# The last batch element: output projection by token halves, its first half two value groups sooner, x in halves, and the last output block in two pieces

## The chip, the cores and the metric

The kernel runs on one core of a Trainium2 chip. The core has a matrix engine (TensorE, "PE" in the profile, with its weight loads as "PEld"), a vector engine (VectorE, "DVE"), a scalar engine (ScalarE, "ACT"), GpSimd ("POOL") and a queue engine (SyncE, "SP") that issues nearly all DMAs here. The engines run side by side, each in its own program order, and wait for each other through semaphores. The metric is the device time of one execution in microseconds (us), as the median over runs.

## What is computed

The input x has 8 batch elements of 512 channels and 32 x 32 = 1024 tokens, in float32. Each element goes through two layers.

```python
# layer 0: group norm, 8-head attention, output projection, group norm, residual
hn  = group_norm(x, gn1_scale, gn1_bias)                       # 32 groups
qkv = einsum('bchw,oc->bohw', hn, w_qkv) + b_qkv
q, k, v = split(qkv.reshape(b * 8, 3 * 64, n))
wgt = softmax(einsum('bct,bcs->bts', q * s, k * s))            # s = 64 ** -0.25
a   = einsum('bts,bcs->bct', wgt, v)
out = einsum('bchw,oc->bohw', a, w_proj) + b_proj
x   = x + group_norm(out, gn2_scale, gn2_bias)
# layer 1: weight-normed attention over tokens, one head of 512 channels
qkv = einsum('oc,bcn->bon', w_qkv, x);  qkv = qkv / (rms(qkv) + 1e-4)
attn = softmax(einsum('bci,bcj->bij', q, k) * 512 ** -0.5)
x   = (x + w_out @ (attn @ v)) * 2 ** -0.5
```

## The kernel before

Channels lie on the 128 partitions in `CI = 4` blocks of 128, tokens in the free dimension; `HN = 512` is half of the tokens. The elements are worked through one after another, and most of what would leave PE idle in one element is filled with work of the next. The last element, b = 7, has no next one, so it has code of its own (the `else` branches of `if more`).

*The attention of layer 0* (`Heads`). The 8 heads are taken in pairs, a pair for each channel block j, and each pair in 8 steps of 128 query tokens, 32 steps in all (`STEPS`). In a step PE makes scores (`s`), DVE takes their maximum, ACT the exponential, POOL scales the rows. One step later `turn` transposes the probabilities on DVE (`pb`, 2.3 us) and issues four DMAs on SP, 256 KB each, that put them in a tile `pT` of the group. Two steps make a group; `values(g)` is the product of the group's `pT` with v (`po`, 32 matmul records of 64 x 256), and ACT copies its result into 256 columns of `a`. A pair has four groups, so groups 12 and 13 are the first half of the tokens of the last pair, and 14 and 15 the second half. Group 13 is taken in the last step, 14 and 15 after it.

*The output projection of the last element.* Output block j is the sum over the four input blocks ci of `proj[ci, j]` times `a[ci]`. `project_out_half` makes the part of ci = 0 and 1 during the last pair's steps, and leaves it in `o`. After `values(14)` and the last `turn`, `OutBegun` makes the part of ci = 2 for j = 0 to 2 in three double-bank PSUM tiles `pp` (tag "sc", three buffers, shared with the scores). `finish_last` adds the part of ci = 3 behind `values(15)`, makes j = 3, and per j DVE adds the tile to `o` over 1024 columns, takes two statistics of 512 columns each (`bn_stats`) and aggregates them. `GroupNorm` turns them into a scale and a shift per channel: two tiny matmuls (`pm`, `pv`) that average over a group, and some twenty small DVE operations. Then for each j ACT scales `o[:, j, :]` and DVE adds it into x, each over 1024 columns. Every matmul of the projection appears as two records in the profile.

*DMAs around it.* SP holds, in this order: the last `turn`'s four DMAs, `score` (weights of layer 1), blocks 2 and 3 of x, then `gram` and `value`. `gram` goes into the buffer in which `proj` lies, so its DMA waits for the last `pp`.

*Layer 1* (`Layer1`). `py` multiplies `gram` with x, block by block, for the norm of q, k and v; `p_u`, `p_v` and `p_e` follow, then `po` (here 128 x 512) with `esum` as the denominators. `products(th, c)` makes output block c of token half th, and `keep` multiplies it by the denominators' reciprocals on DVE, adds x, and for th = 1 issues the whole block's DMA to the output (128 x 1024, 512 KB).

*Buffers.* `Slots` hands out seven large SBUF slots in the order in which they were given back. `wide` takes a double-bank PSUM tile, `bank` a single-bank one (tag "mm", two buffers).

Of the kernel before, what the change touches and what calls it, by code (L numbers as in the profile page):

```python
# [8 lines left out]
F32 = mybir.dt.float32  # L9
I32 = mybir.dt.int32  # L10
AF = mybir.ActivationFunctionType
ALU = mybir.AluOpType
AX = mybir.AxisListType
P = 128
# [4 lines left out]
G1S, G1B, BQ, BK, BV, BP, G2S, G2B, GQKV, GOUT, NCOLS = 0, 4, 8, 12, 16, 20, 24, 28, 32, 44, 48  # L19
# [6 lines left out]
class InOrder:  # L26


    def __init__(self, tc, engine):
        self._pin, self._engine = tc.keep_in_program_order, engine  # L30
# [22 lines left out]
def attention_blocks_kernel(  # L53
# [26 lines left out]
    B, C, H, W = x.shape  # L80
    N = H * W
    NH, D, GROUPS = 8, C // 8, 32
    CI, NT, HN = C // P, N // P, N // 2
# [6 lines left out]
    ov = out.rearrange("b (ci p) h w -> b p ci (h w)", p=P)  # L90

    const = ctx.enter_context(tc.tile_pool(name="const", bufs=1))
    slots = Slots(ctx.enter_context(tc.tile_pool(name="slots", bufs=1)), "s", 7)
# [5 lines left out]
    small = ctx.enter_context(tc.tile_pool(name="small", bufs=3))  # L99
# [4 lines left out]
    PE, VE, AC, PO, SY = (InOrder(tc, e) for e in (nc.tensor, nc.vector, nc.scalar, nc.gpsimd, nc.sync))  # L104

    def big(name, lead=CI):

        return slots.take([P, lead, CI * N // lead], name)

    def wide(name):  # L110
        return ps_s.tile([P, 2, HN], F32, tag="sc", name=name)
# [4 lines left out]
    def matmuls(pm, terms):  # L116

        for k, (lhsT, rhs) in enumerate(terms):
            PE.matmul(pm, lhsT, rhs, start=(k == 0), stop=(k == len(terms) - 1))
            if k % 2:  # L120
                yield

    def run(pieces):
        for _ in pieces:
            pass
# [24 lines left out]
    def load_x(b, xt, ci):  # L150
        SY.dma_start(out=xt[:, ci, :], in_=xv[b, :, ci, :])
# [35 lines left out]
    cols = const.tile([P, NCOLS], F32, name="cols")  # L187
# [18 lines left out]
    def rsqrt(r, v, n, name):  # L206
# [11 lines left out]
    far = {  # L218
        name: dram.tile(shape, F32, tag=f"far_{name}", name=f"far_{name}")
        for name, (_, shape) in places.items()  # L220
        if name not in ("qk", "t24", "qk7", "v", "spare")
    }
# [3 lines left out]
    near = {}  # L226
    far_rinv = dram.tile([NT, P], F32, tag="far_rinv", name="far_rinv")

    def place(name, b):
        tag, shape = places[name]  # L230
        near[name] = weights.tile(shape, F32, tag=f"w_{tag}", name=f"{name}_{b}")
        if name == "v":

            near["v7"] = near[name]
            flat = near[name].rearrange("p k h c -> p (k h c)")
            near["v#"], near["v_"] = flat[:, CI * C :], flat[:, : CI * C]
            near[name] = flat[:, : CI * C].rearrange("p (ci c) -> p ci c", ci=CI)
        return near[name]
# [13 lines left out]
    def fetch(name, b):  # L252
        SY.dma_start(out=place(name, b), in_=far[name])
# [16 lines left out]
    def gn_stats(st, src, k):  # L270
        VE.bn_stats(st[:, k, :], src[:, k * HN : (k + 1) * HN])

    class GroupNorm:


        def __init__(self, mv, n, g0, b0, name, bank=bank):
            self.mv, self.n, self.g0, self.b0, self.name, self.bank = mv, n, g0, b0, name, bank
# [238 lines left out]
    def project_v7(b, right, v):  # L516

        w = near["v7"]

        def unit(m):  # L520
            c = {f"{i + 1}{th + 1}": v[:, m + 4 * th, i * CH : (i + 1) * CH] for i in range(2) for th in range(2)}
            return Seven(
                f"v0_{b}_{m}", CH,
                lambda k, h: w[:, k, h, :], right(slice(m * P, (m + 1) * P)), c, lambda which: None, swap=True,
            ).steps()

        for m in (0, 2):
            units = [unit(m), unit(m + 1)]
            for _ in range(7):
                for u in units:  # L530
                    next(u)
                    yield
# [97 lines left out]
    def out_terms(a, j, th, cis):  # L630
        hs = slice(th * HN, (th + 1) * HN)
        return [(near["proj"][:, ci, j * P : (j + 1) * P], a[:, ci, hs]) for ci in cis]
# [7 lines left out]
                AC.activation(o[:, j, th * HN : (th + 1) * HN], pm, AF.Identity, bias=col(BP, j))  # L640
            yield

    class OutBegun:


        def __init__(self, b, h):
            self.pm = {}
            for j in range(CI - 1):
                self.pm[j] = wide(f"pp_{b}_{j}")
                for th in range(2):  # L650
                    for lhsT, rhs in out_terms(h.a, j, th, [CI // 2]):
                        PE.matmul(self.pm[j][:, th, :], lhsT, rhs, start=True, stop=False)

    def finish_last(b, h, xt, o, begun):

        def project_out(j, th, pm):
            terms = out_terms(h.a, j, th, range(CI // 2, CI))
            if j in begun.pm:  # L660
                PE.matmul(pm[:, th, :], *terms[1], start=False, stop=True)
            else:
                run(matmuls(pm[:, th, :], terms))

        st = small.tile([P, CI, 2, 6], F32, tag="gn_st2", name=f"st2_{b}")
        mv = small.tile([P, CI, 2], F32, tag="gn_mv2", name=f"mv2_{b}")
        for j in range(CI):
            pm = begun.pm[j] if j in begun.pm else wide(f"pp_{b}_{j}")
            for th in range(2):
                project_out(j, th, pm)  # L670
            VE.tensor_add(o[:, j, :], o[:, j, :], pm.rearrange("p a f -> p (a f)"))
            for k in range(2):
                gn_stats(st[:, j], o[:, j, :], k)
            VE.bn_aggr(mv[:, j, :], st[:, j])
        fetch("gram", b)
        norm = GroupNorm(mv, CI, G2S, G2B, f"2_{b}")
        norm.means()
        a, c = norm.coeffs()
        for j in range(CI):
            AC.activation(o[:, j, :], o[:, j, :], AF.Identity, bias=c[:, j : j + 1], scale=a[:, j : j + 1])  # L680
            VE.tensor_add(xt[:, j, :], xt[:, j, :], o[:, j, :])
        slots.give(f"a_{b}")
        slots.give(f"o_{b}")

    class RightSide:

# [197 lines left out]
    class Layer1:  # L884
# [172 lines left out]
        def keep(self, th, c):  # L1057
# [6 lines left out]
            if th == 1:  # L1064
                SY.dma_start(out=ov[self.b, :, c, :], in_=self.xt[:, c, :])

# [2 lines left out]
    gram = place("gram", 0)  # L1072
# [79 lines left out]
    score, value = done1[:, :CI, :], done1[:, CI:, :]  # L1152
# [45 lines left out]
    heads, norm1, hn_next = Heads(0, x0, v0_0, qk0), None, None  # L1198
# [3 lines left out]
    for b in range(B):  # L1202
        hn, more = heads.hn, b + 1 < B
        todo, due, rest = iter(()), [], []
        for i in range(STEPS):
            j, r = divmod(i, NB)
# [13 lines left out]
            if r == 0:  # L1220
# [6 lines left out]
                if j + 1 == CI:  # L1227
                    slots.give(f"hn_{b}")
                    if not more:
                        o_last = big(f"o_{b}")  # L1230
# [5 lines left out]
            if not b:  # L1236
# [9 lines left out]
                k = i - 3 * CI - 2  # L1246
# [16 lines left out]
            if more and m >= 0:  # L1263

                if m < 2:
                    k = slice(2 * (i - STEPS + NB), min(2 * (i - STEPS + NB) + 2, 7))
# [7 lines left out]
            if not more and i == STEPS - 4:  # L1274
                xt = big(f"x_{b}")
# [4 lines left out]
        if more:  # L1280
            v0_next = big(f"v0_{b + 1}", NT)
            v0 = project_v7(b + 1, right_v.columns, v0_next)
            Seven.hold()
            for _ in range(4):
                next(v0)
        heads.values(STEPS // RG - 2)
        heads.turn()
        if more:
            Seven.drain()
            fetch("proj7", b)  # L1290
            ta = big(f"ta_{b}").rearrange("p (k i) (h n) -> p k i h n", k=2, h=2)
            rhs = RightSide(heads.a, ta[:, 0], ta[:, 1])
            for j in range(CI // 2 + 1):
                rhs.sums(j)
            for _ in range(10):
                next(v0)
        else:
            fetch("score", b)
            begun = OutBegun(b, heads)
            for ci in (2, 3):  # L1300
                load_x(b, xt, ci)
        heads.values(STEPS // RG - 1)
        slots.give(f"v0_{b}")
        if more:
            xt = big(f"x_{b}")
            for ci in range(CI):
                load_x(b, xt, ci)
            fetch("gram", b)
            finish_layer0(b, heads, rhs, xt, v0)
        else:  # L1310
            finish_last(b, heads, xt, o_last, begun)
        fetch("value", b)
        one = Layer1(b, xt)
        one.project(hn_next)
# [27 lines left out]
        if more:  # L1342
            one.products(1, 0, norm_step)
            run(steps)
            one.keep(1, 0)
            heads = Heads(b + 1, hn_now, v0_next, qk_next)
            heads.scores(0)
            fills = [[lambda c=c: one.products(1, c)] for c in range(1, CI)] + [[]]
            laters = [[lambda c=c: one.keep(1, c)] for c in range(1, CI)] + [[]]

            def done(b=b):
                for name in (f"v1_{b}", f"e_{b}_1", f"x_{b}"):
                    slots.give(name)

            laters[CI - 2].append(done)
        else:
            for c in range(CI):
                one.products(1, c)
                one.keep(1, c)


# [31 lines left out]
```

## Time and profile before

| what | value |
| --- | --- |
| time, median of 3 runs | 3246.95 us (3246.25 to 3247.75) |
| the profiled execution: time / span of its core | 3249.17 / 3246.7 us |
| granted TensorE clock, mean | 0.998 |
| PE busy | 3217.5 us (99%), 13346 matmul records |
| DVE busy | 2274.4 us (70%) |
| ACT busy | 1045.7 us (32%) |
| POOL busy | 1253.0 us (39%) |
| PE, DVE, ACT busy in 3056 to 3068 us | 2.01, 8.75, 2.69 of 12 us |

How to read it: the span is the time from the first to the last instruction of the core; the execution's own time is 2.47 us longer. The profile's pages give groups by engine and operation as "out<-in", with the mean duration of one in ns. The chain of waits follows the work that ended last back from the last instruction, at each step to what released it. A timeline row has its start and duration in us, the engine, the operation, its tiles and shapes, a count where equal instructions were merged, and in brackets the idle time before it with what ended it. Nearly all operations are recorded on line 34 (a helper), so tiles tell them apart. Matmul ends are modelled.

### The profile page before, as it was taken

What the parts mean: (1) busy time and instruction counts of PE and PEld (TensorE: products, weight loads), DVE (VectorE), ACT (ScalarE), POOL (GpSimd) and SP (SyncE); (2) the same over time, 40 slices, a digit from 0 to 9 for tenths busy, and PEclk for the clock granted to TensorE, in tenths of its full rate; (3) what the DMA queues carried; (4) which work ended last, traced back from release to release, by engine and by line L of the source; (5) the groups of instructions that cost most, each with busy time, mean ns of one, the idle gap of its engine ahead of it and who ended that gap; (6) DMA issues with size and microseconds to landing.
All of it is one profiled execution on the core that took longest, in us unless ns stands there. A gap on an engine that the chain in (4) does not pass through costs nothing.

```text
span 3246.7 us, 36723 instructions
## 1 busy us (share of the span) xinstructions
PE 3217.5 (99%) x13346; PEld 1657.8 (51%) x13346; DVE 2274.4 (70%) x3074; ACT 1045.7 (32%) x1813; POOL 1253.0 (39%) x1025
## 2 busy tenths in 40 slices
PE   8999999999999999999999999999999999999899
PEld 5445644455444554445544555445554456444454
DVE  5697667876678756886668866687667876578643
ACT  2453114521145211551215412254123531145210
POOL 1554224732257212671227603265223642246121
PEclk9999999999999999999999999999999999999999
DMA  6776215862168511784228822388214872158500
GB/s 201 213 203 209 75 49 155 219 193 59 49 183 229 171 43 56 202 229 138 52 77 214 229 96 63 95 219 242 78 49 115 216 214 75 23 157 210 183 7 26
DMA packets 231579, 447.34 MB, mean 138 GB/s; under 512 B 28996, under 2 KB 69480, under 8 KB 225512
## 3 DMA queue, kind: packets, MB, share of 16 engines
q1 hardware_dynamic: 231280, 444.97, 49.0%
q8 instruction: 107, 1.75, 0.2%
q14 instruction: 72, 0.59, 0.1%
q10 hardware_dynamic: 120, 0.02, 0.0%
HBM read 133.06 MB, written 29.52 MB: 50 GB/s over the span
## 4 chain that ended last, share of the span: by engine, by line
PE 93%; DMA 3%; DVE 2%; SPq 1%; issue 1%; POOL 0%; DVEq 0%
PE po L34 26%; PE s L34 13%; PE pq L34 7%; PE p_e_T L34 7%; PE p_v_T L34 6%; PE p_e_B L34 5%; PE p_v_B L34 5%; PE py L34 4%; PE pqk L34 4%; PE p_u_T L34 3%; PE p_o_T L34 3%; DMA pT<-pb 3%; PE p_u_B L34 3%; PE p_o_B L34 2%; SPq L34 1%; DVE pb L34 1%
## 5 line engine op out<-in xcount | busy, mean ns | idle before, releaser
L34 POOL TENSOR_SCALAR p<-p,tt 128x1024 f32<-128x1024 f32 x512 | 565.9, 1118 | 753.7 <-DVE tt L34 734.9
L34 ACT ACTIVATE p<-s,nm 128x1024 f32<-128x1024 f32 x512 | 565.7, 1109 | 887.7 <-DVE nm L34 794.1
L34 DVE TENSOR_REDUCE nm<-s 128x1 f32<-128x1024 f32 x512 | 602.0, 1217 | 158.9 <-PE s L34 158.6
L34 DVE STREAM_TRANSPOSE pb<-p 128x2048 f32<-128x2048 f32 x256 | 589.6, 2303 | 45.6 <-DMA pT<-pb 20.8
L34 PE MATMUL s<-qk 64*128 64x512 f32 x2048 | 526.5, 604 | 0.6
L34 PE MATMUL po<-pT,v 128*64 128x256 f32 x4096 | 471.7, 383 | 3.5 <-DMA pT<-pb 3.4
L34 PE MATMUL po<-e,v 128*128 128x512 f32 x1024 | 451.7, 595 | 0.0
L34 PEld LDWEIGHTS po<-pT,v 128*64 128x64 f32 x4096 | 285.9, 137 | 220.8 <-ACT v L34 32.6
L34 PEld LDWEIGHTS s<-qk 64*128 64x128 f32 x2048 | 199.5, 186 | 253.3 <-issue 227.9
L34 PEld LDWEIGHTS po<-e,v 128*128 128x128 f32 x1024 | 191.9, 190 | 245.0 <-issue 236.4
L34 POOL TENSOR_TENSOR u<-u,xy 128x512 f32<-128x512 f32 x64 | 78.9, 1270 | 335.4 <-DMA xy<-far_rinv 261.4
L34 PE MATMUL pq<-hn,qk 64*128 64x512 f32 x504 | 197.1, 592 | 0.0
L34 POOL TENSOR_TENSOR esum<-esum,e 128x512 f32<-128x512 f32 x96 | 130.5, 1360 | 154.2 <-ACT e L34 151.7
L34 POOL TENSOR_TENSOR x<-x,o 128x1024 f32<-128x1024 f32 x21 | 52.1, 2512 | 348.3 <-ACT o L34 348.3
L34 ACT ACTIVATE e<-e,shift,rinv 128x512 f32<-128x512 f32 x128 | 100.9, 812 | 256.6 <-DVE e L34 256.6
L34 DVE TENSOR_TENSOR e<-e,p_e_T 128x512 f32<-128x512 f32 x160 | 106.9, 684 | 86.5 <-PE p_e_T L34 84.3
L34 DVE TENSOR_TENSOR v<-v,p_v_T 128x256 f32<-128x256 f32 x300 | 114.2, 415 | 68.7 <-PE p_v_T L34 50.0
L34 PE MATMUL pqk<-hn,qk 64*128 64x512 f32 (+1 forms) x672 | 158.2, 590 | 0.0
L34 PE MATMUL pq<-t,qk 64*128 64x512 f32 x336 | 150.9, 589 | 0.0
L34 PE MATMUL pq<-v,qk 64*128 64x512 f32 x336 | 150.9, 589 | 0.0
L34 PE MATMUL p_e_T<-s,t 128*128 128x512 f32 x320 | 147.8, 592 | 0.0
L34 PE MATMUL py<-x,gram 128*128 128x512 f32 x320 | 140.2, 597 | 5.4 <-issue 5.4
(215 smaller groups left out, 4130.9 us busy)
## 6 DMA issues: line engine op xcount, KB each, us to landing
pT<-pb SPq DMA_DIRECT2D x1024, 256.0 KB, 4.4
qk<-far_qk SPq DMA_DIRECT2D x21, 896.0 KB, 8.6
hn<-in_x_dram SPq DMA_DIRECT2D x32, 512.0 KB, 5.8
x<-in_x_dram SPq DMA_DIRECT2D x32, 512.0 KB, 4.5
out_dram<-x SPq DMA_DIRECT2D x32, 512.0 KB, 3.8
score<-far_score SPq DMA_DIRECT2D x8, 1792.0 KB
value<-far_value SPq DMA_DIRECT2D x8, 1792.0 KB, 7.2
proj<-far_proj SPq DMA_DIRECT2D x7, 1792.0 KB
```

The lines of the kernel that those rows point to most:

```text
L34: return lambda *args, **kw: self._pin(call(*args, **kw))
```

## The change

All of it concerns the last element.

1. `LastOut` takes the place of `OutBegun` and `finish_last`. Its PSUM tiles hold two output blocks of one token half instead of two halves of one block. `first_half` makes the parts of ci = 2 and 3 for tokens 0 to 511, right after `values(13)` and ahead of `values(14)`. `sums` adds one block's half to `o` and takes its statistic: for block 0 it stands ahead of the last `turn` on DVE, for blocks 1 to 3 behind it. `begin_second` makes the part of ci = 2 of the second half ahead of `values(15)`, and `finish` the part of ci = 3 behind it, then the four remaining sums, the aggregates and the norm.
2. ACT's scaling and DVE's addition into x go by halves of 512 columns.
3. `gram` goes into one of the seven slots, and its DMA is issued ahead of x's blocks 2 and 3 and `score`.
4. The last output block's first half is sent on its own; its second half is made, scaled and sent in two pieces of 256 columns.

```diff
-    class OutBegun:
...
-    def finish_last(b, h, xt, o, begun):
...
+    class LastOut:
+        def __init__(self, b, h, o):
...
+        def two(self, th, js):
+            t = wide(f"pp_{self.b}_{th}_{js[0]}")
+            for k, j in enumerate(js):
+                self.pm[th, j] = t[:, k]
+        def share(self, th, j, ci, first):
+            for lhsT, rhs in out_terms(self.h.a, j, th, [ci]):
+                PE.matmul(self.pm[th, j], lhsT, rhs, start=first, stop=not first)
+        def first_half(self):
+            for js in ((0, 1), (2, 3)):
+                self.two(0, js)
+                for j in js:
+                    self.share(0, j, CI - 2, True)
+                    self.share(0, j, CI - 1, False)
+        def sums(self, th, j):
+            oh = self.o[:, j, th * HN : (th + 1) * HN]
+            VE.tensor_add(oh, oh, self.pm[th, j])
+            VE.bn_stats(self.st[:, j, th, :], oh)
+        def begin_second(self):
+            for js in ((0, 1), (2, 3)):
+                self.two(1, js)
+                for j in js:
+                    self.share(1, j, CI - 2, True)
+        def finish(self, xt):
+            for j in range(CI):
+                self.share(1, j, CI - 1, False)
+            for j in range(CI):
+                self.sums(1, j)
+                VE.bn_aggr(self.mv[:, j, :], self.st[:, j])
+            norm = GroupNorm(self.mv, CI, G2S, G2B, f"2_{b}")
+            norm.means()
+            a, c = norm.coeffs()
+            for j in range(CI):
+                for th in range(2):
+                    hs = slice(th * HN, (th + 1) * HN)
+                    AC.activation(
+                        o[:, j, hs], o[:, j, hs], AF.Identity, bias=c[:, j : j + 1], scale=a[:, j : j + 1]
+                    )
+                    VE.tensor_add(xt[:, j, hs], xt[:, j, hs], o[:, j, hs])
...
+        def last_piece(self, c, cols):
+            hs, po = slice(HN + cols.start, HN + cols.stop), bank(f"po1_{self.b}_1_{c}_{cols.start}", HN // 2)
+            run(matmuls(po, [(self.v[:, t, c * P : (c + 1) * P], self.e[1][:, t, cols]) for t in range(NT)]))
+            VE.tensor_mul(po, po, self.sums[1][:, cols])
+            VE.scalar_tensor_tensor(self.xt[:, c, hs], self.xt[:, c, hs], 2.0 ** -0.5, po, ALU.mult, ALU.add)
+            SY.dma_start(out=ov[self.b, :, c, hs], in_=self.xt[:, c, hs])
...
+        else:
+            last = LastOut(b, heads, o_last)
+            last.first_half()
+            last.sums(0, 0)
         heads.values(STEPS // RG - 2)
         heads.turn()
...
         else:
-            fetch("score", b)
-            begun = OutBegun(b, heads)
+            for j in range(1, CI):
+                last.sums(0, j)
+            last.begin_second()
+            near["gram"] = big(f"gram_{b}")[:, :, :C]
+            SY.dma_start(out=near["gram"], in_=far["gram"])
             for ci in (2, 3):
                 load_x(b, xt, ci)
+            fetch("score", b)
         heads.values(STEPS // RG - 1)
...
-            finish_last(b, heads, xt, o_last, begun)
+            last.finish(xt)
...
-            for c in range(CI):
+            for c in range(CI - 1):
                 one.products(1, c)
                 one.keep(1, c)
+            SY.dma_start(out=ov[b, :, c + 1, :HN], in_=xt[:, c + 1, :HN])
+            for n in (0, HN // 2):
+                one.last_piece(c + 1, slice(n, n + HN // 2))
```

More of the change, by code (lines that the diff above doesn't have):

```diff
@@ L641, in project_out_half @@
             yield
-    class OutBegun:
-        def __init__(self, b, h):
-            self.pm = {}
-            for j in range(CI - 1):
-                self.pm[j] = wide(f"pp_{b}_{j}")
-                for th in range(2):
-                    for lhsT, rhs in out_terms(h.a, j, th, [CI // 2]):
-                        PE.matmul(self.pm[j][:, th, :], lhsT, rhs, start=True, stop=False)
-    def finish_last(b, h, xt, o, begun):
[L658 to L683, printed above, removed]
@@ new lines, in attention_blocks_kernel @@
+    class LastOut:
+        def __init__(self, b, h, o):
+            self.b, self.h, self.o = b, h, o
+            self.st = small.tile([P, CI, 2, 6], F32, tag="gn_st2", name=f"st2_{b}")
+            self.mv = small.tile([P, CI, 2], F32, tag="gn_mv2", name=f"mv2_{b}")
+            self.pm = {}
+        def two(self, th, js):
[21 more added lines that the diff above has]
+        def finish(self, xt):
+            b, o = self.b, self.o
+            for j in range(CI):
[7 more added lines that the diff above has]
+            for j in range(CI):
+                for th in range(2):
+                    hs = slice(th * HN, (th + 1) * HN)
[3 more added lines that the diff above has]
+                    VE.tensor_add(xt[:, j, hs], xt[:, j, hs], o[:, j, hs])
+            slots.give(f"a_{b}")
+            slots.give(f"o_{b}")
```

## The prediction

> **What bounds the kernel now.** I read the page first, then the chain of waits over the last 250 us, then the timeline of single engines where that chain leaves PE. By the page, the chain that ended last is
>
> ```profile
> PE 93%; DMA 3%; DVE 2%; SPq 1%; issue 1%; POOL 0%; DVEq 0%
> ```
>
> So TensorE sets the time, and a change that takes no matmul away can gain only where the chain is not on PE. The chain over the last batch element shows one such place that is long (columns: start us, duration us, what):
>
> ```profile
> 3044.29 3.67 PE po L34 x32
> 3047.97 1.93 PE pp L34 x4
> 3049.89 0.02 issue
> 3049.92 1.23 DVE o L34
> ...
> 3060.44 0.22 DVE mv L34
> ...
> 3062.53 5.38 issue
> 3067.91 18.88 PE py L34 x40
> ```
>
> From 3049.92 to 3067.91 us the chain is DVE and ACT: no later element is left whose work could fill PE. Of these 18.0 us, 10.7 are the sums of the output projection and their statistics (3049.92 to 3060.66), 4.65 the group norm's small operations, and 2.60 the scaling and the first addition into x. The DVE timeline shows what one of four channel blocks costs, and how long DVE stood idle just before:
>
> ```profile
> 3034.35 2.31 DVE L34 STREAM_TRANSPOSE pb<-p 128x2048 f32<-128x2048 f32 x1 [2.34 <-POOL p L34]
> 3049.92 1.22 DVE L34 TENSOR_TENSOR o<-o,pp 128x1024 f32<-128x1024 f32 x1 [13.25 <-PE pp L34]
> ...
> 3057.91 1.17 DVE L34 TENSOR_TENSOR o<-o,pp 128x1024 f32<-128x1024 f32 x1
> 3059.11 1.29 DVE L34 BATCH_NORM_STATS2 st<-o 128x6 f32<-128x512 f32 x2
> 3060.44 0.21 DVE L34 BATCH_NORM_AGGREGATE mv<-st 128x2 f32<-128x12 f32 x1
> ```
>
> From py on, PE is busy without a break to the last matmul (chain, 3067.91 to 3241.52). Behind it only this tail counts:
>
> ```profile
> 3241.54 0.70 DVE L34 TENSOR_TENSOR po<-po,esum 128x512 f32<-128x512 f32 x1 [5.45 <-PE po L34]
> 3242.27 0.69 DVE L34 SCALAR_TENSOR_TENSOR x<-x,po 128x512 f32<-128x512 f32 x1
> 3242.99 0.33 SPq L34 DMA_DIRECT2D out_dram<-x  x1
> ```
>
> The span ends at 3246.70, 3.71 us after that DMA's issue.
>
> **Part 1: half of the sums leave the chain (−4.4 us).** DVE now does, per block, an addition over 1024 columns (1.20 us to the next start), two statistics (1.32) and an aggregate (0.13), 2.65 us, four times. After the change, first-half additions and statistics stand before the last values group, in the idle 13.25 us above: four additions of 128x512 (0.69, the x<-x,po row) and four statistics (0.68, the row's mean), 5.6 us with their gaps. What is left is, per block, 0.72 + 0.71 + 0.13 = 1.56 us, with the last aggregate 6.32 us. 10.74 − 6.32 = 4.42 us.
>
> **Part 2: what the move costs in front (+1.9 us).** The 32 pp matmul records after group 13 stay 32; 16 of them now stand before group 14, 8 before group 15, 8 at the end. Group 13 starts at 3027.29 and holds PE 3.61 us (the step from one group to the next matmul elsewhere), so the first pp starts at 3030.90 in a gap that PE now spends waiting for group 14's transposed tile ([2.83 <-DMA pT<-pb] at 3033.80). At 0.43 us a record, with 0.11 for ACT's copy of group 13 (ready 3031.48), 16 records end at 3037.9; with 0.19 at each change of operand group 14 starts at 3038.1, long after its tile, and the 8 further records at 3041.7. PE can start group 15 at 3045.3, against 3044.29: **+1.0**.
>
> The catch is DVE's order. The addition for block 0 stands before the last transpose on DVE, and in the instruction order of the changed kernel it waits for the last of the four products of its PSUM tile, blocks 0 and 1 both. These 8 records end at 3034.6; the addition and its statistic hold DVE until 3036.0, so the transpose starts at 3036.0 instead of 3034.35. Queued behind it are its four SP DMAs, and group 15 waits for those. Before, the last of them landed 7.5 us after the transpose ended (3044.20, just ahead of the 3044.29 start); for the transpose before that it took 6.4. So the tile lands between 44.8 and 45.9. I take PE's 3045.3, because the earlier transpose's DMAs, which shared the engines with these, will by then be done; the upper end adds 0.6.
>
> At the end the same pairing counts: block 0's addition must wait for four records behind ACT's copy of group 15, not two: 2 × 0.43 = **+0.86**. DVE's sums then start at 3045.3 + 5.63 + 0.86 = 3051.8 and end at 3058.1, 2.5 us earlier than now.
>
> **Part 3: x in halves (−1.1 us).** ACT's first scaling takes 1.23 us and DVE follows 0.05 later; a 128x512 ACT operation takes 0.63 to 0.81 in this trace (squares, exponentials), so I take 0.70. DVE's addition goes from 1.22 to 0.68, and py starts 0.10 after it: 0.75 + 0.68 + 0.10 = 1.53 instead of 2.60. The other seven pieces come every 0.7 us while py's first matmuls are slow (below), so PE does not wait for them. py starts at 3064.4, 3.5 us earlier.
>
> **Part 4: the last block in two pieces (−1.4 us).** PE's share is unchanged: 128x256 matmuls step by 0.215 us (p_v: 16 in 3.45), 512-wide ones by 0.43. The last two DVE operations become 256 wide (0.42, the p_v additions): 1.42 to 0.87 us. The last DMA carries 128 KB instead of 512. Its 128 packets, eight on each engine, shrink from 4 KB (0.159 us in the packet records) to 1 KB (between 0.027 for 512 B and 0.084 for 2 KB, so 0.045): about 0.9 of 3.71 us. Bounds: 0 (all of it fixed) and 1.3. The two earlier pieces and block 2 leave SP 3 us or more ahead.
>
> **Free edits.** gram goes to a slot that group 13 frees, and is issued first, then x's blocks 2 and 3, score and value: 5.8 MB. At 292 GB/s (what 3036 to 3048 moved) gram and x are in by 3051, score by 3058, value by 3064; first uses are near 3064, 3083 and 3109. Landing at 3068 instead would cost 3.6 us.
>
> **The sum.** +1.02 + 0.86 − 4.42 − 1.07 − 1.42 = −5.0 us. The profiled execution has a span of 3246.70 and a time of 3249.17, which becomes 3244.2; the median of the runs, 2.2 us below it, goes from 3246.95 to 3242.0 (−0.15%).
>
> **The clock.** After PE's idle stretch, weights for py's first records come every 0.86 us, then every 0.43:
>
> ```profile
> 3067.88 0.50 PEld L34 LDWEIGHTS py<-x,gram 128*128 128x128 f32 x2 [5.45 <-issue]
> 3068.90 0.34 PEld L34 LDWEIGHTS py<-x,gram 128*128 128x128 f32 x1 [0.52 <-issue]
> ...
> 3071.18 0.19 PEld L34 LDWEIGHTS py<-x,gram 128*128 128x128 f32 x1 [0.24 <-issue]
> ```
>
> These 3.0 slow us cost 1.5 (18.72 us from py to p_u_B, against 40 × 0.43 = 17.2). The sum leaves them as they are. [...]
>
> **Rivals.**
> A, the slow stretch of py shrinks: at most 1.5 us more, together with an early landing in the tail (0.4 more) 6.9 saved, 3240.0. [...] Against: PE is idle about as long before py as now.
> B, it grows by as much: 3.5 saved, 3243.5. [...]
> C, the change does not do what it says: the first-half sums slip behind group 15 because DVE or PSUM is late, and nothing is gained but the tail and x halves: 2.5 − 1.9 saved, 3246.3. Against: 13.25 idle us of DVE, and PSUM tiles whose readers end 1 us before they are wanted.
> D, slower: group 15's tile. The transpose is 1.7 us late and gram and x now follow its DMAs directly. If their 2.1 MB (7.2 us at 292 GB/s) shared the engines with it instead of following, the tile would land at 3044.8 + 7.2 = 3052.0, 6.7 after PE is ready, and a PE idle that long would run group 15 slow as it ran group 14 (5.11 us in the chain against 3.67): −5.0 + 6.7 + 1.4 = 3.1 slower, 3250.1. It decides from a landing at 3049 on. For it: the 2.83 us wait for group 14 shows such tiles can be late. Against: score's 1.8 MB followed the same DMAs before, and group 15 did not wait.
>
> **Numbers.** Forecast 0.68 (3240.6 to 3243.0), A 0.14, B 0.11, C 0.04, D 0.03. The range 3240.0 to 3244.2 takes in the bounds of parts 2 and 4 and both clock cases, and leaves out C, D and the far ends. A change of 0.2%, about what a measurement of this kernel can tell from none, is 6.5 us: faster by more than that is A and the best edge of the forecast, 0.17; slower is D where it is worse than worked out, 0.02; within it the rest, 0.81.
>
> **What would show it.** Right: pp x16 directly behind group 13 with no wait for pT before group 14; the last transpose near 3036.0; DVE's last sums 6.3 us long, starting near 3051.8; py near 3064.4; last DVE operations of 0.42 and less than 3 us behind the last issue. Wrong: a transpose at 3034.4 (the pairing is not real), a wait for pT before group 15 over 0.6 us, first-half sums after group 15, py waiting for gram, or a py stretch other than 18.7 us.

## The result and the profile after

Over 20 runs of each kernel the median went from 3249.26 us (3245.87 to 3253.99) to 3244.38 us (3241.66 to 3249.58). The ratio is 0.9986, with a 95% interval of 0.9979 to 0.9992: 4.5 us faster, 2.6 to 6.8. The forecast was −5.0 us, −0.15%, so the difference lies where it was put. The time itself does not: 3244.38 is 0.2 us above the range given, because the kernel before is not at 3246.95, the median of the three runs shown, but 2.3 us higher.

The profiled execution of the changed kernel has a span of 3243.2 us and a time of 3245.3. Its chain over the last element (start us, duration us, what):

```profile
3030.69 7.06 PE pp L34 x16
3037.75 3.60 PE po L34 x32
3041.36 3.63 PE pp L34 x8
3044.99 0.76 issue
3045.74 3.69 PE po L34 x32
...
3049.98 2.00 PE pp L34 x4
...
3052.01 0.70 DVE o L34
...
3058.02 0.22 DVE mv L34
...
3063.02 0.82 ACT o L34
...
3063.87 0.70 DVE x L34
...
3064.61 19.91 PE py L34 x40
```

PE goes straight from group 13 into pp and has no gap ahead of group 14. There is a new one, 0.76 us, ahead of group 15; the last transposed piece of its tile lands at 3045.65 by the trace's DMA records, so the nameless wait is a DMA's. DVE's last sums run from 3052.01 to 3058.24, 6.2 us instead of 10.7. py comes 3.3 us sooner, but takes longer: 19.75 us to p_u_B instead of 18.72.

The DVE timeline shows why group 15's tile is late:

```profile
3034.36 0.69 DVE L34 TENSOR_TENSOR o<-o,pp 128x512 f32<-128x512 f32 x1 [2.62 <-PE pp L34]
3035.08 0.69 DVE L34 BATCH_NORM_STATS2 st<-o 128x6 f32<-128x512 f32 x1
3035.69 2.29 DVE L34 STREAM_TRANSPOSE pb<-p 128x2048 f32<-128x2048 f32 x1
```

DVE waits 2.62 us for pp, and the transpose stands behind that: it starts 8.7 us after group 13 instead of 7.1. In the tail, the last two DVE operations and the last issue are

```profile
3239.31 0.43 DVE L34 TENSOR_TENSOR po<-po,esum 128x256 f32<-128x256 f32 x1 [2.56 <-PE po L34]
3239.78 0.42 DVE L34 SCALAR_TENSOR_TENSOR x<-x,po 128x256 f32<-128x256 f32 x1
3240.23 0.33 SPq L34 DMA_DIRECT2D out_dram<-x  x1
```

and the span ends at 3243.22, 2.99 us behind that issue (3.71 before).

### The profile page after: what moved, and what is told of

It reads as the page before. It is cut to its first block, busy times and chain, and to the rows that moved or that the text cites. A ratio compares the mean times of both kernels' runs of the same rounds, so it can differ in the third digit from the quotient of the medians.

```text
span 3243.2 us, 36769 instructions
## 1 busy us (share of the span) xinstructions
PE 3216.9 (99%) x13362; PEld 1662.9 (51%) x13362; DVE 2277.4 (70%) x3084; ACT 1047.8 (32%) x1817; POOL 1254.4 (39%) x1025
## 4 chain that ended last, share of the span: by engine, by line
PE 93%; DMA 3%; DVE 2%; SPq 1%; issue 0%; POOL 0%; ACT 0%; DVEq 0%; ACTq 0%
PE po L34 26%; PE s L34 13%; PE p_e_T L34 7%; PE pq L34 7%; PE p_v_T L34 6%; PE p_e_B L34 5%; PE p_v_B L34 5%; PE py L34 4%; PE pqk L34 4%; PE p_u_T L34 3%; PE p_o_T L34 3%; PE p_u_B L34 3%; DMA pT<-pb 2%; PE p_o_B L34 2%; DVE pb L34 1%; SPq L34 1%
## 5 line engine op out<-in xcount | busy, mean ns | idle before, releaser
L34 PE MATMUL po<-e,v 128*128 128x512 f32 (+1 forms) x1040 | 451.7, 589 | 0.0
```

The costliest lines, as they stand in the source:

```text
L34: return lambda *args, **kw: self._pin(call(*args, **kw))
```

## The experiments

All of them leave the part ahead of group 13 of the last element as it was. So each profile gives two numbers: when group 13 starts, and the *stretch*, from there to the end of the span. The stretch is 219.4 us in the profile of before, and 216.2 in that of the change.

**The kernel before, again.** No edit.

> The kernel before, unchanged. Theory 1 (the forecast's steps were right and its starting level was low: executions of this kernel differ by several us, and three of them gave a median on the low side): a ratio of 1.000 within 0.001, single times spread over 3246 to 3254 us, and a profile in which the stretch from the start of values group 13 of the last element to the last DVE operation is the 215.7 us of the earlier profile within 1.5 us, while the start of group 13 may lie anywhere from 3025 to 3034 us. Rival (the level is steady and the loss was in the changed stretch): single times within 1.5 us of 3247, group 13 starts within 0.5 us of 3027.3.

Measured: ratio 1.0002 (0.9993 to 1.0011), single times 3246.7 to 3252.8; the kernel before had a median of 3249.0 over 33 runs beside it. In the profile group 13 starts at 3024.09, 3.2 us sooner than in the first, and the stretch is 220.2. The rows of PE at the place of the change:

```profile
3030.39 3.67 PE L34 MATMUL po<-pT,v 128*64 128x256 f32 x32 [2.63 <-DMA pT<-pb]
...
3040.65 3.67 PE L34 MATMUL po<-pT,v 128*64 128x256 f32 x32 [1.24 <-DMA pT<-pb]
```

Theory 1 holds: the level moves, and it moves ahead of the changed code (group 13 is even 0.9 us outside the band that was named for it). In the twelve profiles of this study group 13 starts between 3024.09 and 3031.60 us, 7.5 us apart, with the same instructions in front of it. Note the second row: in the kernel before, too, group 15 can wait for its tile.

**The tail alone.** The kernel before with `last_piece` as in the change, and its calls:

```diff
...
-            for c in range(CI):
+            for c in range(CI - 1):
                 one.products(1, c)
                 one.keep(1, c)
+            SY.dma_start(out=ov[b, :, c + 1, :HN], in_=xt[:, c + 1, :HN])
+            for n in (0, HN // 2):
+                one.last_piece(c + 1, slice(n, n + HN // 2))
```

> The kernel before with the last output block in two pieces and nothing else of the change. By the forecast: last DVE operations 0.87 us instead of 1.42, from the last DMA's issue to the end of the span 2.8 instead of 3.7, together 1.4 us sooner, ratio 0.9996. Rival (the DMA's time is fixed whatever its size): 0.55 us sooner, the span ending 3.7 us behind the issue.

Measured: ratio 0.9996 (0.9988 to 1.0005), which alone cannot be told from no change. The profile can: last DVE operations 0.89 us instead of 1.42, and from the last issue at 3243.42 to the end of the span 2.70 us instead of 3.71. Together that is 1.5 us, and the fixed-time rival is out. The stretch is 218.2.

**x in halves alone.**

```diff
-            AC.activation(o[:, j, :], o[:, j, :], AF.Identity, bias=c[:, j : j + 1], scale=a[:, j : j + 1])
-            VE.tensor_add(xt[:, j, :], xt[:, j, :], o[:, j, :])
+            for th in range(2):
+                hs = slice(th * HN, (th + 1) * HN)
+                AC.activation(o[:, j, hs], o[:, j, hs], AF.Identity, bias=c[:, j : j + 1], scale=a[:, j : j + 1])
+                VE.tensor_add(xt[:, j, hs], xt[:, j, hs], o[:, j, hs])
```

> The kernel before with ACT's scaling and DVE's addition into x by halves and nothing else. By the forecast: from ACT's first scaling to py's first matmul 1.5 to 1.6 us instead of 2.60, py itself 18.7 us if its slow stretch keeps its length; 1.0 us sooner, ratio 0.9997. Rival (the eight pieces hold up py): py's stretch to p_u_B grows by 1 us or more because PE waits for later pieces of x, and nothing is gained. Rival (the granted clock decides): py's stretch takes any length from 17.2 to 20 us, according to where the half-clock stretch ends, with no wait for DVE behind its fourth matmul.

Measured: ratio 0.9995 (0.9987 to 1.0004); from ACT's first scaling to py 1.64 us instead of 2.60, and py to p_u_B 19.04. Weight loads come every 0.86 us until 3068.84 and every 0.43 from 3069.31 on, so the later pieces of x hold nothing up; the end of the slow stretch does not follow them. The third theory fits. The stretch is 217.9, 1.5 to 2.2 less than before, but 0.4 to 0.9 of that is group 15, which starts 16.14 us behind group 13 here (17.0 and 16.56 in the two profiles of before). The edit does not touch that part: here group 15 waits 0.67 us for its tile, in the second profile of before 1.24, and in the first it does not wait, but group 14 takes 5.11 us instead of 3.67, 3.0 of them at half clock (3033.34 to 3036.75 by the clock records).

**The projection alone.** The changed kernel with the loops of the kernel before for x and the tail.

> The changed kernel without x in halves and without the two-piece tail: the projection by token halves and gram's own slot alone. By the forecast's steps with what the changed kernel's profile showed: group 15 starts 18.5 to 18.8 us behind group 13 instead of 17.0, DVE's last sums take 6.2 us instead of 10.7 and start 6.3 us behind group 15 instead of 5.6; py starts 2.3 to 2.6 us sooner relative to group 13, ratio 0.9992. Rival (the late transpose eats the gain): py starts less than 1 us sooner relative to group 13, ratio 1.000.

Measured: ratio 0.9993 (0.9984 to 1.0002). Group 15 starts 18.58 us behind group 13 and now waits for a DMA by name:

```profile
3050.18 3.67 PE L34 MATMUL po<-pT,v 128*64 128x256 f32 x32 [0.60 <-DMA pT<-pb]
```

The sums start 6.26 us behind it and take 6.2; py starts 38.29 us behind group 13, against 40.62 and 40.20: 1.9 to 2.3 us, at or a little under the lower end of what was expected. The stretch is 217.2. The three ratios of the parts, 0.9996, 0.9995 and 0.9993, add up to 0.9984, the whole measured 0.9986; each of the three is uncertain by 0.0009, so what each part is worth is read from its profile.

**The transpose first.**

```diff
             last.first_half()
-            last.sums(0, 0)
...
-            for j in range(1, CI):
+            for j in range(CI):
                 last.sums(0, j)
```

> The changed kernel with the sums of block 0's first half behind the last transpose on DVE instead of ahead of it. Theory (the late transpose makes group 15's tile late): the transpose starts 7.0 to 7.2 us behind group 13's start as in the kernel before (8.7 in the changed kernel), group 15 starts when PE is free, 18.0 to 18.1 us behind group 13 instead of 18.7, and the stretch from group 13's start to the end of the span falls from 216.2 to about 215.5 us. Rival (the DMAs behind the tile, gram and x, hold it up): group 15 still waits and starts 18.5 us or more behind group 13 with the transpose at 7.1.

Measured: ratio 0.9983 (0.9974 to 0.9991). DVE's and PE's rows:

```profile
3032.18 2.31 DVE L34 STREAM_TRANSPOSE pb<-p 128x2048 f32<-128x2048 f32 x1 [2.35 <-POOL p L34]
...
3043.02 3.67 PE L34 MATMUL po<-pT,v 128*64 128x256 f32 x32
```

The transpose is back at 7.1 us behind group 13 (3025.11), where POOL ends its wait as before, and group 15 starts at 17.9 with no wait, though only just: the last piece of its tile lands at 3042.92 by the DMA records. So the 0.6 to 0.8 us there came from the order on DVE, not from gram or x. The stretch is 214.7, 0.8 below the expectation, of which py's length explains 0.7 (19.04 instead of the 19.75 that was counted on).

**Own PSUM tiles for blocks 0 and 1.**

```diff
-            for js in ((0, 1), (2, 3)):
+            for js in ((0,), (1,), (2, 3)):
                 self.two(0, js)
...
-            for js in ((0, 1), (2, 3)):
+            for js in ((0,), (1,), (2, 3)):
                 self.two(1, js)
```

> The changed kernel with blocks 0 and 1 of each half in PSUM tiles of their own, so that an addition waits for its own block's products alone. Theory (both costs in front come from the shared tile): the transpose starts 7.0 to 7.2 us behind group 13, group 15 18.0 to 18.1 us, DVE's last sums start 5.6 us behind group 15 instead of 6.26; group 13 to the end of the span about 214.9 us instead of 216.2. Rival (group 15 waits for the DMAs anyway, or PSUM is short with six tiles in three buffers): only the 0.6 us at the sums, or PE waits for DVE ahead of group 15.

Measured: ratio 0.9974 (0.9964 to 0.9985). DVE's and PE's rows (group 13 starts at 3026.92):

```profile
3032.54 0.69 DVE L34 TENSOR_TENSOR o<-o,pp 128x512 f32<-128x512 f32 x1 [0.91 <-PE pp L34]
...
3033.98 2.31 DVE L34 STREAM_TRANSPOSE pb<-p 128x2048 f32<-128x2048 f32 x1
...
3044.82 3.67 PE L34 MATMUL po<-pT,v 128*64 128x256 f32 x32
```

The first addition starts 5.6 us behind group 13 instead of 7.4 and the transpose 7.06; group 15 starts at 17.9 without a wait; the last sums start 5.41 us behind it (0.2 sooner than expected). The stretch is 214.8 as expected, although py met its longest slow time, 20.03. Against the change: group 15 0.8 sooner, the sums 0.85, py 0.3 longer.

**PE kept busy.** Nine products that nobody reads:

```diff
+            idle = wide(f"idle_{b}")
+
+            def keep_busy(n):
+                for _ in range(n):
+                    PE.matmul(idle[:, 0], near["proj"][:, 0, :P], self.h.a[:, 0, :HN], start=True, stop=True)
+
+            keep_busy(5)
             norm = GroupNorm(self.mv, CI, G2S, G2B, f"2_{b}")
             norm.means()
             a, c = norm.coeffs()
+            keep_busy(4)
```

> The changed kernel with nine more products of 128x512 into a spare PSUM tile that nobody reads, five behind the last pp and four behind pv: work that stands in PE's idle time and changes no output. Theory (the granted clock falls to half in that idle time, and py starts in it): no half-clock stretch there, py to p_u_B 17.2 to 17.6 us instead of 19.75 in the changed kernel's profile (18.7 to 19.9 in the others), py no later than now; group 13 to the end of the span 213.7 to 215.0 us instead of 216.2. Rival (the slow first py matmuls wait for x in pieces, not for the clock): py to p_u_B stays over 18.7 us. Rival (the added products are in the way): pm, pv or py start later by 0.5 us or more.

Measured: ratio 0.9980 (0.9971 to 0.9989). PE's rows:

```profile
3053.82 4.46 PE L34 MATMUL idle<-a,proj 128*128 128x512 f32 x10
3058.68 0.36 PE L34 MATMUL pm<-mv,gavg 128*128 128x4 f32 x2 [0.40 <-DVE mv L34]
3059.77 0.36 PE L34 MATMUL pv<-d,gavg 128*128 128x4 f32 x2 [0.73 <-DVE mean L34]
3059.98 3.68 PE L34 MATMUL idle<-a,proj 128*128 128x512 f32 x8
3064.51 17.43 PE L34 MATMUL py<-x,gram 128*128 128x512 f32 x40 [0.85 <-DVE x L34]
3081.78 1.88 PE L34 MATMUL p_u_B<-x,score 128*128 128x512 f32 x4
```

py to p_u_B is 17.27 us, the 40 × 0.43 of full speed, and the mean granted clock of the run is 1.0 instead of 0.998. The records of pm and pv shrink too, 0.36 us instead of 0.56, and from pm's second record to ACT's scaling it takes 4.14 instead of 4.45. The stretch is 213.1, 0.6 below the expectation's lower end, which had left pm and pv out. x in pieces is not what slows py's start: with the granted clock at 1.0, py's weight loads come every 0.43 us from 3065.91 on.

**Both together.**

> Both of the last two: own PSUM tiles for blocks 0 and 1, and PE kept busy behind the last pp and behind pv. If the two costs are independent, group 13 to the end of the span is 212.5 to 213.5 us (216.2 less 1.3 and less 1.5 to 2.4), ratio to the kernel before 0.9979 with the spread of the part ahead of group 13 on top, so 0.997 to 0.999. Rival (they overlap, since an earlier py meets another clock state): no better than the better one alone.

Measured: ratio 0.9970 (0.9959 to 0.9982), median 3240.17 us of 6 runs beside 3248.62. Stretch 211.9, 7.5 to 8.3 below the kernel before and 3.4 to 4.3 below the change. That is 0.6 under the expected range, again by pm and pv. Against the first profile of the change 4.3 us are saved. The two edits alone save 1.7 (own tiles, with py's length left out) and 3.1 (PE kept busy), so the two costs are nearly independent. Some 0.3 us are lost again: pm starts 0.45 us behind the last aggregate instead of 0.14, directly behind the idle products, of which five are too many once the sums end sooner. This version is the fastest of the study by ratio and by stretch; against the change as it stands the two intervals overlap, and the claim rests on the stretch.

**gram in its old place.** The changed kernel with `fetch("gram", b)` behind the sums, `score` and x ahead of it, as before the change.

> The changed kernel with gram back in proj's buffer, so that its DMA waits for the last pp and stands behind score and x. Theory (the forecast: gram's move costs and brings nothing, its cover is wide): gram is issued near 27 us behind group 13's start and lands 5 us later, py still waits for DVE's x alone; group 13 to the end of the span as in the changed kernel, 215.2 to 217 us. Rival (py waits for gram): py's idle time ends with a DMA, 1 us or more later. Rival (gram's packets held up group 15's tile): group 15 starts 18.0 us behind group 13 instead of 18.5 to 18.7.

Measured: ratio 0.9982 (0.9973 to 0.9991), gram issued at 3052.31, 26.5 us behind group 13. py's wait still ends with DVE's x, group 15 still starts at 18.53, and the stretch is 214.9, 0.3 under the expected range (py was 18.68). gram's move shows no effect here, good or bad.

**The change, again.** No edit.

> The changed kernel once more. Theory (the changed stretch is steady and the part ahead of it is not): from group 13 to the end of the span 215.0 to 217.0 us, whatever the time at which group 13 starts (3024 to 3032 us in the other profiles); ratio 0.9986 within 0.001, single times spread over 3241 to 3250 us. Rival (the changed stretch is what varies): group 13 near 3027 us and a stretch more than 1.5 us away from 216.2.

Measured: ratio 0.9985 (0.9976 to 0.9994), single times 3240.2 to 3246.9. Group 13 starts at 3024.36 and the stretch is 215.3: 0.9 off the first profile, which is py (18.87 instead of 19.75).

## Why the forecast was right in its difference and wrong in its time

Where the terms came out, from the two first profiles:

| step | forecast, us | measured, us |
| --- | --- | --- |
| group 13 to group 15 | +1.0 (to +1.6) | +1.7 (17.00 to 18.73) |
| pairs at the end | +0.86 | +0.64 (5.62 to 6.26) |
| from the sums' start to pm's second record | −4.4 | −4.4 (11.01 to 6.57) |
| from there to ACT's scaling | 0 | +0.1 |
| x in halves | −1.07 | −1.0 (2.60 to 1.59) |
| py to p_u_B | 0 | +1.0 (18.72 to 19.75) |
| tail | −1.42 | −1.25 |
| sum | −5.0 | −3.2 |

Group 13 itself started 0.3 us sooner, which makes the 3.5 us between the spans.

That the difference came out so close to −5.0 is partly luck. Without py, whose length differs from one execution to the next (below), the steps of the table add up to −4.2, and the interval of 2.6 to 6.8 us holds either.

**The step that failed is the last line of the sum, the level.** The forecast went from the profiled execution's 3249.17 back to 3246.95 by "2.2 us below it", and laid its range around that. The three runs agreed within 1.5 us, and the range took that for their uncertainty. Twenty runs of the kernel before have a median of 3249.26, the 33 beside the first experiments 3249.0, with 8 us between the lowest and the highest; the profiled execution's 3249.17 is close to both medians. Laid on 3249.26, the same −5.0 gives 3244.3, and 3244.38 was measured. The range held the bounds of the changed steps, but nothing for the part ahead of the change, which varies by more than all of them.

What makes that part vary is only partly shown. Between the two profiles that are farthest apart (the kernel before again, and the projection alone), PE's waits ahead of 3024 us that are named differ by 2.8 us: 1.4 on a transposed tile, 1.0 on POOL's additions into qk, 0.4 on ACT. Part of the other 4.7 us of the 7.5 is hidden in rows that count as busy: the same 12746 matmul records ahead of group 13 are busy for 3013.4 us in the one profile and 3017.9 in the other. Three groups of scores (near 2138, 2925 and 2996 us of the second) lose nearly 1 us each against the first, with a weight load inside that waits for ACT's exponentials (p). Why ACT is late there is not known, and no run here took a cause away.

**Part 1** was right in size and place. **Part 2** had the mechanism right, a transpose behind an addition that waits for a pair of blocks, and the shared tile is shown to be its cause by the experiment with own tiles. Its size was too small, +1.7 where +1.0 was taken and +1.6 allowed: the value taken, PE's 3045.3, supposed that the transpose's DMAs would be quicker once the earlier ones were done. They were not. The last piece landed 7.7 us after the transpose ended, as against 7.5 in the profile of before, although the earlier transpose's pieces had all landed by 0.6 us after that end. Of the 7.7, 3.3 us pass until SP has issued the fourth DMA, 4.4 from there to its landing. The 6.4 that the prediction has for the transpose before does not come out of the landing records, which give 7.1, and for the last three transposes of all twelve profiles 6.7 to 8.8. The one profile of before was not typical either: with the old order group 15 starts 16.1 to 17.2 us behind group 13 in four profiles, with the changed order 18.5 to 18.7 in five, so the move costs about 1.9 us on average. **Parts 3 and 4** hold within 0.2 us.

**The clock** was left as it is in the sum, and rival B was what the profile of the change shows. By the trace's clock records half clock was granted from 3060.64 to 3070.89 in the profile of before and from 3055.99 to 3069.64 in that of the change, 10.24 and 13.65 us, of which 3.0 and 5.0 lie behind py's start (3067.91 and 3064.61). Over all profiles with the idle gap py took 18.7 to 20.0 us, with and without the change (18.72 and 19.90 in two profiles of the kernel before). So B is no effect of the change but a difference between executions, worth up to 1.3 us; the forecast had set it down as a way in which the change could go. From py's start to the end of the slow stretch it was 3.0 us in one profile of the kernel before and 5.4 in the other; what sets that end is not shown. That the idle time is the cause of the slow stretch is shown by the run in which PE was kept busy: the mean granted clock was 1.0 there instead of 0.998, and py took 17.27 us.

**Rivals and signs.** Of the prediction's signs of being wrong two came: group 15 waited 0.76 us for its tile (over 0.6), and py's stretch was 19.75 instead of 18.7; its signs of being right came as well. A did not come: py's stretch never fell under 18.7 us while PE idled ahead of it. C did not: the first-half sums ended at 3041.9, ten microseconds ahead of the second half's. D's place was right, its price was not: group 15 waited 0.56 to 0.76 us for its tile in every profile of the changed order, and no less (0.56) with score directly behind it in gram's place. That group 15 did not wait in the kernel before, the argument against D, was the luck of one profile: in the second it waited 1.24 us.

## What to carry to other kernels

When a single unhidden chain is shortened, forecast the difference from the profile, and take the level, and its spread, from as many runs as there are: three close runs were no measure of it here. Work moved ahead of an instruction on the same engine delays all that hangs on that instruction (here the transpose, 8.7 us behind group 13 instead of 7.1); look at what the first moved operation waits for, and note that an accumulator tile which two results share makes the first wait for the second (here the first addition stood 7.4 us behind group 13, and 5.6 with own tiles). The gap in the matrix engine's work ahead of py cost twice here, once as a gap and once as a slow start behind it (py took 18.7 to 20.0 us); where such a gap cannot be closed, idle products in it can take the second cost away, as they did here (17.27 us).

## What the runs showed of the hardware that was not expected

- With the same instructions ahead of it, the last element's group 13 starts anywhere from 3024.09 to 3031.60 us; the stretch behind it differs by only 0.8 us between the two profiles of the kernel before and by 0.9, nearly all of it py's length (19.75 and 18.87), between the two of the change.
- Half clock came already in a wait of PE of 2.83 us: in the profile of before it was granted from 3033.34 to 3036.75, and group 14, which started at 3033.80 behind that wait, took 5.11 us instead of 3.67. In the tail alone it took 5.36 us behind a wait of 2.49. In the other two profiles with such a wait, the kernel before again and x in halves alone, it took 3.67 behind 2.63 and 2.77 us, so the length of the wait alone does not decide it; what does is not shown. It cost little ahead of group 14, since the next group's tile landed only about when PE was ready for it (3044.20 in the profile of before, where group 15 starts at 3044.29).
- The span ended 2.7 to 3.0 us behind the issue of a last store of 128 KB, and 3.7 behind one of 512 KB.
